# One core, four conditioned residual blocks: when ScalarE may read a bank of the first block, and how many units of the other work a step of the recurrence takes when that work is late

## The chip, the cores and the metric

The kernel runs on one core of a Trainium2 chip. The metric is the device time of one execution, in microseconds (us). Three runs of the kernel before the change took 1317.85 to 1319.22 us, with a median of 1318.93 us. One more execution was profiled; it took 1318.28 us, and its profile spans 1316.5 us from the first to the last instruction.

## The reference

The input is x of 8 sequences, 512 positions and 256 features, with one condition vector per sequence. Four residual blocks follow each other, x = x + block(x):

```
L0  s    = sigmoid(x @ router_w.T + cond @ router_t_w.T);  the two best of 8 experts, gates normalized
    out  = (silu(x @ sw1.T) * (x @ sw3.T)) @ sw2.T  +  sum_e gate_e * gelu(x @ rw1_e.T) @ rw2_e.T
    x    = x + out / 3
L1  a Haar transform scaled by gate(cond) and back: x * (a factor per sequence and feature)
L2  mid  = gelu(x @ base_down + (low rank, generated from cond));  x = x + mid @ base_up + (low rank)
L3  a GRU over the 512 positions, H of 8 x 256:
    Z = sigmoid(xz + H Whz), R = sigmoid(xr + H Whr), C = tanh(xh + (R*H) Whh), H = Z*H + (1-Z)*C
    x = x + H Whq + bhq
```

L0 to L2 treat every position by itself. L3 is a chain of 512 steps, each of which needs the one before.

## The kernel before

**Windows.** The 512 positions are cut into 16 windows of 32 (all 8 sequences together: 256 columns). `window_jobs` (line 497) writes down, for one window, everything of L0, L1 and L2 as a list of jobs; it runs nothing. Each job has an engine, the jobs that it depends on, the buffers that it uses and an assumed duration (`TAKES`). A product of 128 x 128 weights with 256 columns is one job of TensorE; `quads` (line 482) issues it as four matmuls of 32 output columns each. Such a job is called a unit (or a quad) here. In the profile every one of these matmuls has line 485, and a unit shows as x8 instructions, since a float32 matmul is recorded as two.

**Banks.** A hidden layer's tile in PSUM has 2 halves of 256 columns and fills one bank of 2 KB per partition (`r_h`, two of them; in window 0 every third one is `low`). `hidden` (line 557) makes the two units of one half. For the shared expert (lines 575 to 605) the first half holds x sw1 (units j0, j1) and the second x sw3 (j2, j3); ScalarE takes the sigmoid of the first half (line 583, tile `sig`) and VectorE makes two products (lines 591 and 599, tiles `lin` and `g`). For the routed experts (lines 607 to 642) the halves are two experts; ScalarE takes erf of each (line 617), VectorE makes `gl` (line 625), GpSimd multiplies by the gate that a DMA has spread over the partitions (line 634, tiles `bc` and `g`). `into_acc` adds two units per part to the window's sum `acc`. The framework orders accesses to PSUM by the bank, so a matmul into the second half that stands behind ScalarE's read of the first half in the program waits for that read.

**Two ways of ordering.** Ahead of the recurrence, `Jobs.run` (line 181) plays a clock in steps of 0.02 us and gives every engine the first job of its queue that is ready by the assumed durations; this carries windows 0 and a part of 1, the routing of the first four windows (`route`, line 903: logits on TensorE, some 25 small VectorE instructions, a transpose `cT` at line 939, a DMA to `comb_d` in DRAM at line 990, and from there by DMA into `bc` at line 517), the small products for the condition (line 1034) and the generation of the low-rank weights (`misc`, line 1104), which consumes eight loads of 1 MB. An engine's instructions are then issued in just this order, and each engine executes in order.

In the recurrence (lines 1362 to 1491) a step is written out by hand: the products of H for r and z on TensorE (line 1197, tiles `grh` and `gz`), ScalarE's gates (line 1379, `r`, `z`, `c`), VectorE's transposes (line 1393), the product R*H (line 1410), the products for the candidate (line 1197 with `s_rh`) and the scan that makes the new H (line 1469). Between them stand slots for the jobs of the windows. `first_slot` (line 1334) says how many units TensorE takes between the z products and the candidate's products, `second_slot` (line 1342) how many after those. `behind(s, by)` (line 1328) says whether more units are left than a straight line from the start to about step 462 allows, by more than `by`. In the first slot a late kernel takes a unit only if more than one is ready; in the second it takes two instead of one if the work is 8 units late (or late at all, in every second step) and more than two are ready. While window 1 isn't done (the first steps), both take what there is.

Of the kernel before, what the change touches and what calls it, by code (L numbers as in the profile page):

```python
# [18 lines left out]
KC = C // P  # L19
E = 8  # L20
# [40 lines left out]
PE_ALONE, PE_WOVEN = 0.43, 0.65  # L61
LEAD = 20
AHEAD = 1
RATE = 0.36
LAG = 3.5

# [137 lines left out]
def cond_resid_kernel(  # L204
# [173 lines left out]
    def load_sw13(k):  # L378
# [10 lines left out]
    rw1_sb = const.tile([P, KC, E, P], F32, name="rw1_sb")  # L389
    half = slice(0, E // 2), slice(E // 2, E)  # L390
    got_rw1 = [
        load(
            rw1_sb[:, :, e],
            rw1.rearrange("(k p) (e h) -> p k e h", p=P, h=P)[:, :, e],
            0.5,
        )
        for e in half
    ]
# [98 lines left out]
    def window_jobs(w, routed, xt, via_pool=False):  # L497

        add = jobs.add
        x = xw[w]  # L500

        def mm(lazy, n, lhs, rhs, start, deps, reads=(), tiles=NQ, takes=None):

            return add(
                "PE",
                lambda: quads(lazy.get()[: 32 * tiles, n], lhs(), rhs(), start, tiles),
                deps,
                [lazy, *reads],
                takes,
            )  # L510

        bcs = [Lazy(r) for r in r_bc]

        def fetch(i):
            (nc.gpsimd if via_pool else nc.sync).dma_start(
                out=bcs[i].get(),
                in_=comb_d[w : w + 1, 2 * i : 2 * i + 2].broadcast_to([P, 2, NT]),
            )  # L520

        fetched = [
            add(
                "POOL" if via_pool else "SP",
                lambda i=i: fetch(i),
                [routed[w % EARLY], got_w2 if w == 1 else None],
                [bcs[i]],
                1.0 if via_pool else None,
                lag=1.4 * LAG if via_pool else LAG,
            )  # L530
            for i in range(E // 2)
        ]

        acc = Lazy(r_acc)
        order = [None]

        def into_acc(part, lhs, deps, got):
            for m in range(KC):
                first = order[0] is None
                order[0] = mm(  # L540
                    acc,
                    m,
                    lambda m=m: lhs()[:, ts(m, P)],
                    lambda: part.get(),
                    first,
                    [*deps, got, order[0]],
                    [part],
                )

        turn = [0]  # L550

        def bank():

            turn[0] += 1
            return Lazy(r_low if w == 0 and turn[0] % 3 == 0 else r_h)

        def hidden(lazy, n, lhs, got, first=None):

            made = []
            for k in range(KC):  # L560
                made.append(
                    mm(
                        lazy,
                        n,
                        lambda k=k: lhs(k),
                        lambda k=k: x[:, k],
                        k == 0 and first is None,
                        [first, *made, got[k], got_x[w][k]],
                    )
                )  # L570
            return made

        later = []

        for m in range(HC):
            h, sig, lin, g = bank(), Lazy(r_sig), Lazy(r_lin), Lazy(r_g)
            j0, j1 = hidden(h, 0, lambda k, m=m: sw13_sb[:, k, 0, ts(m, P)], got_sw13)
            *_, j3 = hidden(
                h, 1, lambda k, m=m: sw13_sb[:, k, 1, ts(m, P)], got_sw13, j0
            )  # L580
            a = add(
                "ACT",
                lambda h=h, sig=sig: nc.scalar.activation(  # L583
                    sig.get(), h.get()[:, 0], AF.Sigmoid
                ),
                [j1],
                [h, sig],
            )
            d = add(
                "DVE",  # L590
                lambda h=h, sig=sig, lin=lin: tt(
                    lin.get(), h.get()[:, 0], sig.get(), ALU.mult
                ),
                [j1, a],
                [h, sig, lin],
            )
            d = add(
                "DVE",
                lambda h=h, lin=lin, g=g: tt(g.get(), h.get()[:, 1], lin.get(), ALU.mult),
                [j3, d],  # L600
                [h, lin, g],
            )
            later.append((g, lambda m=m: sw2_sb[:, m], [d], got_sw2))
            if len(later) > 2:
                into_acc(*later.pop(0))

        for e2 in range(0, E, 2):
            h, j0 = bank(), None
            for n in range(2):
                e = e2 + n  # L610
                got = [got_rw1[e // (E // 2)]] * KC
                j = hidden(h, n, lambda k, e=e: rw1_sb[:, k, e, :], got, j0)
                j0, j = j
                sig, gl, g = Lazy(r_sig), Lazy(r_gl), Lazy(r_g)
                a = add(
                    "ACT",
                    lambda h=h, sig=sig, n=n: nc.scalar.activation(  # L617
                        sig.get(), h.get()[:, n], AF.Erf, scale=RSQRT2
                    ),
                    [j],  # L620
                    [h, sig],
                )
                d = add(
                    "DVE",
                    lambda h=h, sig=sig, gl=gl, n=n: stt(
                        gl.get(), sig.get(), 1.0, h.get()[:, n], ALU.add, ALU.mult
                    ),
                    [j, a],
                    [h, sig, gl],
                    queue=None if w else jobs.small,  # L630
                )
                p = add(
                    "POOL",
                    lambda gl=gl, g=g, e=e: nc.gpsimd.tensor_tensor(  # L634
                        g.get(), gl.get(), bcs[e // 2].get()[:, e % 2], ALU.mult
                    ),
                    [d, fetched[e // 2]],
                    [gl, g, bcs[e // 2]],
                )
                later.append((g, lambda e=e: rw2_sb[:, e], [p], got_rw2))  # L640
                if len(later) > 3:
                    into_acc(*later.pop(0))
        for part in later:
            into_acc(*part)
        l0_ends.append(order[0])


        x1, x2, mid = Lazy(r_x1), Lazy(r_x2), Lazy(r_mid)
        turned = []
        halves = 2 if w < HALVED else 1  # L650
        for half in range(halves):
            at = slice(half * WS // halves, (half + 1) * WS // halves)
            turned.append(lower(w, at, acc, x1, x2, mid, xt, order[0]))
        return turned
# [184 lines left out]
    mu, j = mean_over_features(cond, got_cond)  # L839
    diff = set1.tile([P, KC, B], F32, name="diff")  # L840

    def center():
        for k in range(KC):
            tt(diff[:, k, :], cond[:, k, :], mu.get()[:, :B], ALU.subtract)

    j = dve(center, [j], [mu], 0.4)
    dsq = set1.tile([P, KC, B], F32, name="dsq")
    j = dve(lambda: tt(dsq, diff, diff, ALU.mult), [j])
    var_ps, j = mean_over_features(dsq, j)
    var = set1.tile([P, B], F32, name="var")  # L850
    j = dve(
        lambda: nc.vector.tensor_scalar(var, var_ps.get()[:, :B], EPS_LN, None, ALU.add),
        [j],
        [var_ps],
    )
# [5 lines left out]
    j = dve(  # L861
        lambda: tt(
            prod,
            rout[:, 1].rearrange("p k (o e) -> p k o e", o=1).broadcast_to([P, KC, B, E]),
            cond.rearrange("p k (b o) -> p k b o", o=1).broadcast_to([P, KC, B, E]),
            ALU.mult,
        ),
        [got_cond, got_rout],
    )
# [12 lines left out]
    j = pe(time_bias, [j], [tb_ps])  # L882
# [198 lines left out]
    for n, of in enumerate(LOW):  # L1081
# [15 lines left out]
        for k in range(KC):  # L1097
            got = [pieces[q, k] for q in of]
# [69 lines left out]
    with (  # L1168
# [159 lines left out]
        def behind(s, by=0):  # L1328
            return (
                any(j.done is None for j in ends[1][0])  # L1330
                or jobs.left("PE") > all_left * (LAST - s) / (LAST + LEAD) + by
            )

        def first_slot(s, at):

            if any(j.done is None for j in ends[1][0]) or jobs.ending() and jobs.left("PE"):
                return 1
            if jobs.left("PE"):
                return 1 if behind(s) and jobs.ready("PE", at + 1.0) > 1 else 0
            return 1 if len(jobs.last["PE"]) > T - s else 0  # L1340

        def second_slot(s, at):

            if not jobs.left("PE"):
                return 1
            two = behind(s, 8) or (s + 5) % 2 == 0 and behind(s)
            if two and (any(j.done is None for j in ends[1][0]) or jobs.ending()):
                return 2
            return 2 if two and jobs.ready("PE", at + 1.0) > 2 else 1
# [212 lines left out]
```

## Time and profile before

| what | us |
| --- | --- |
| median of three runs | 1318.93 |
| the profiled execution | 1318.28 |
| its span, first to last instruction | 1316.5 |
| before the first gate of step 0 (ScalarE's first `r`) | 67.77 |
| 511 steps from there to the first gate of the last step | 1241.18 |
| the rest: last step, last outputs | 7.55 |

The last three rows are read from the rows `ACT L1379 ACTIVATE r<-grh` of the trace, of which each step has two. The page gives per engine the busy time; TensorE is busy for 1178.3 us (89%), VectorE for 916.8 (70%), ScalarE for 505.7 (38%), GpSimd for 150.6 (11%). A row of the timeline gives start and duration in us, the engine (PE is TensorE's matmul, PEld its weight load, DVE VectorE, ACT ScalarE, POOL GpSimd, SPq the DMA queue that SyncE issues to), the line, the operation, output and input tiles, how many instructions are merged, and in brackets how long the engine was idle before and what released it. "issue" as a releaser means that the engine waited for nothing that the profile shows.

### The profile page before, as it was taken

Reading aid. Unit: us, or ns where it says so; the run is one execution under the profiler, and the core shown is the slowest. Engines: PE = TensorE matmul, PEld = TensorE weight load, DVE = VectorE, ACT = ScalarE, POOL = GpSimd, SP = SyncE. Lnnn points to the kernel's source line nnn. Section 1 sums busy time; section 2 is a strip of 40 time slices with the busy share of each in tenths; the row PEclk is TensorE's granted clock in tenths of the full one; section 3 lists DMA queues with packets and bytes.
Section 4 is the critical chain, followed back from the end, with each engine's and each line's share of the span. In section 5 each row is a group of like instructions: output and inputs, shape, how many; then the busy total and the mean of one; then the engine's idle time right before and its main releaser. Section 6 shows DMA issues by size and latency. Waiting matters only on the chain.

```text
span 1316.5 us, 88999 instructions
## 1 busy us (share of the span) xinstructions
PE 1178.3 (89%) x39240; PEld 688.4 (52%) x39240; DVE 916.8 (70%) x6271; ACT 505.7 (38%) x3407; POOL 150.6 (11%) x235
## 2 busy tenths in 40 slices
PE   8999999899999999998888988888888888878886
PEld 5666555555555555555554555545554545545443
DVE  5367777777776767676776767677676767667775
ACT  2134343444344444334343433443434344433332
POOL 3311110101011110101011010101101011110000
PEclk9999999999999999999999999999999999999999
DMA  9910001200010010100000010000001000000111
GB/s 318 352 53 16 5 4 38 52 5 29 13 36 20 12 29 5 52 4 28 12 15 26 4 36 4 22 19 12 28 4 29 12 4 4 4 4 4 36 30 26
DMA packets 41859, 46.46 MB, mean 35 GB/s; under 512 B 27488, under 2 KB 31104, under 8 KB 40320
## 3 DMA queue, kind: packets, MB, share of 16 engines
q1 hardware_dynamic: 38576, 38.31, 9.5%
q8 instruction: 306, 5.01, 1.6%
q0 software_dynamic: 1184, 2.31, 0.5%
q14 instruction: 81, 0.66, 0.2%
q10 hardware_dynamic: 1712, 0.16, 0.1%
HBM read 36.45 MB, written 4.33 MB: 31 GB/s over the span
## 4 chain that ended last, share of the span: by engine, by line
PE 66%; DVE 19%; ACT 9%; issue 4%; DMA 2%; SPq 0%; ACTq 0%
PE grh L1197 35%; PE hp L485 11%; DVE d L1393 7%; DVE rT L1393 6%; PE acc L485 6%; PE gz L1197 5%; ACT c L1379 5%; PE low L485 4%; ACT r L1379 4%; PE misc L485 3%; DVE s_h L1469 3%; DVE s_rh L1410 2%; DMA bc<-comb_d 1%; DMA sw_sb<-in_sw_dram 0%; PE misc L1104 0%
## 5 line engine op out<-in xcount | busy, mean ns | idle before, releaser
L1393 DVE STREAM_TRANSPOSE rT<-r 128x32 f32<-128x32 f32 x1024 | 156.1, 191 | 219.5 <-ACT r L1379 215.8
L1379 ACT ACTIVATE r<-grh 128x32 f32<-128x32 f32 x1024 | 146.3, 195 | 421.0 <-PE grh L1197 418.2
L1197 PE MATMUL grh<-wh,s_h 128*32 128x64 f32 x8192 | 221.8, 225 | 90.1 <-DVE s_h L1469 89.1
L1197 PEld LDWEIGHTS grh<-wh,s_h 128*32 128x32 f32 x8192 | 140.4, 109 | 309.6 <-DVE s_h L1469 308.4
L1379 ACT ACTIVATE c<-grh 128x32 f32<-128x32 f32 x1024 | 146.2, 195 | 313.6 <-PE grh L1197 313.1
L1197 PE MATMUL grh<-wh,s_rh 128*32 128x64 f32 x8192 | 221.6, 225 | 34.3 <-DVE s_rh L1410 10.0
L1197 PEld LDWEIGHTS grh<-wh,s_rh 128*32 128x32 f32 x8192 | 139.2, 108 | 191.8 <-DVE s_rh L1410 188.1
L1393 DVE STREAM_TRANSPOSE d<-c 128x32 f32<-128x32 f32 x1024 | 156.5, 192 | 115.2 <-ACT c L1379 108.9
L1197 PE MATMUL gz<-wh,s_h 128*32 128x64 f32 x8192 | 209.9, 219 | 0.4 <-issue 0.3
L1197 PEld LDWEIGHTS gz<-wh,s_h 128*32 128x32 f32 x8192 | 153.5, 110 | 0.9 <-issue 0.8
L485 PE MATMUL acc<-g,rw_sb 128*32 128x256 f32 x2048 | 153.5, 379 | 0.0
L485 PE MATMUL hp<-x,sw_sb 128*32 128x256 f32 x2016 | 150.8, 384 | 2.6 <-ACT sig L583 2.2
L634 POOL TENSOR_TENSOR g<-gl,bc 128x256 f32<-128x256 f32 x128 | 93.6, 733 | 511.9 <-DVE s_h L1469 358.8
L485 PE MATMUL hp<-x,rw_sb 128*32 128x256 f32 x2016 | 151.4, 380 | 0.7 <-ACT sig L617 0.6
L1469 DVE TENSOR_TENSOR_SCAN s_h<-d,d 128x16 f32<-128x16 f32 x1024 | 145.4, 184 | 0.0
L1410 DVE TENSOR_TENSOR s_rh<-rT,s_h 128x8 f32<-128x8 f32 x1024 | 133.5, 168 | 0.0
L1393 DVE STREAM_TRANSPOSE zT<-z 128x64 f32<-128x64 f32 x512 | 121.9, 238 | 0.4 <-ACT z L1379 0.3
L1379 ACT ACTIVATE z<-gz 128x64 f32<-128x64 f32 x512 | 121.4, 237 | 0.8 <-PE gz L1197 0.4
L1483 ACT COPY hist<-s_h 128x16 f32<-128x16 f32 x512 | 106.3, 208 | 0.5 <-DVE s_h L1469 0.5
L1197 PE MATMUL grh<-wx,xt 128*32 128x128 f32 x2048 | 104.8, 274 | 1.3 <-ACT r L1379 1.1
L1422 DVE TENSOR_TENSOR d<-zT,s_h 128x16 f32<-128x16 f32 x512 | 90.7, 177 | 17.5
L1423 DVE TENSOR_SCALAR d<-zT 128x16 f32<-128x16 f32 x512 | 86.8, 169 | 0.0
(154 smaller groups left out, 1208.7 us busy)
## 6 DMA issues: line engine op xcount, KB each, us to landing
bc<-comb_d SPq DMA_DIRECT2D x56, 256.0 KB, 3.2
w<-in_w_dram SPq DMA_DIRECT2D x5, 1024.0 KB, 13.5
out_dram<-x SPq DMA_DIRECT2D x14, 256.0 KB, 3.2
x<-in_w_dram SPq DMA_DIRECT2D x3, 1024.0 KB, 15.6
x<-in_xT_dram SPq DMA_DIRECT2D x2, 1536.0 KB
bc<-comb_d POOLq DMA_DIRECT2D x8, 256.0 KB, 9.0
sw_sb<-in_sw_dram SPq DMA_DIRECT2D x3, 512.0 KB, 8.0
wsq_a<-in_sq_a_dram SPq DMA_DIRECT2D x1, 1280.0 KB
```

Of the source, the lines that this page charges most:

```text
L485: nc.tensor.matmul(out[ts(j, 32)], lhs[:, ts(j, 32)], rhs, start=start, stop=False, skip_group_check=True,)
L634: lambda gl=gl, g=g, e=e: nc.gpsimd.tensor_tensor(g.get(), gl.get(), bcs[e // 2].get()[:, e % 2], ALU.mult),
L1197: nc.tensor.matmul(out[ts(j, 32)], lhs, rhs[:, ..., ts(j, FQ)], start=start, stop=False, skip_group_check=True,)
L1379: nc.scalar.activation(x, y, func)
L1393: ins = nc.vector.transpose(dst.rearrange("p i u b -> p i (u b)"), src.rearrange("p (i r) -> p i r", r=32),)
L1410: prod = tt(s_rh[u][:, k, u, :], rT[:, k, u, :], h[:, k], ALU.mult)
L1422: tt(d1[:, :, u, :, 1], zT[:, :, u, :], h, ALU.mult)
L1423: nc.vector.tensor_scalar(d0[:, :, :, 1], zT[:, :, u, :], -1.0, 1.0, ALU.mult, ALU.add)
L1469: new = nc.vector.tensor_tensor_scan(s_h[v][:, k, v].rearrange("p b w -> p (b w)"), d0[:, k].rearrange("p b w -> p (b w)"), d1[:, k, u].re ...
L1483: nc.scalar.copy(hist[:, :, t, :], s_h[v][:, :, v, :, 1])
```

## The change

Three edits. A constant `FAR = 16` is added, as line 64, so that all later lines move by one and more.

In window 0 (`w` is 0) ScalarE's read of a bank depends on the last unit of the bank's second half too, so that it is placed in the program behind both halves; in the other windows its dependencies are as they were.

For the routed experts the list of TensorE's jobs is written in another order, in all windows: the four units of a bank come first, and then what is added to `acc`; before, one part of `acc` stood between the two halves.

In the steps, when the work is more than 16 units late, the first slot takes one unit and the second two if so many are ready, without the conditions on how many are ready.

```diff
+FAR = 16
...
                 lambda h=h, sig=sig: nc.scalar.activation(
                     sig.get(), h.get()[:, 0], AF.Sigmoid
                 ),
-                [j1],
+                [j1, None if w else j3],
                 [h, sig],
...
         for e2 in range(0, E, 2):
-            h, j0 = bank(), None
-            for n in range(2):
+            h, j0, ends = bank(), None, []
+            for e in (e2, e2 + 1):
+                got = [got_rw1[e // (E // 2)]] * KC
+                j0, j = hidden(h, e % 2, lambda k, e=e: rw1_sb[:, k, e, :], got, j0)
+                ends.append(j)
+            for n, j in enumerate(ends):
                 e = e2 + n
-                got = [got_rw1[e // (E // 2)]] * KC
-                j = hidden(h, n, lambda k, e=e: rw1_sb[:, k, e, :], got, j0)
-                j0, j = j
                 sig, gl, g = Lazy(r_sig), Lazy(r_gl), Lazy(r_g)
                 a = add(
                     "ACT",
                     lambda h=h, sig=sig, n=n: nc.scalar.activation(
                         sig.get(), h.get()[:, n], AF.Erf, scale=RSQRT2
                     ),
-                    [j],
+                    [j, None if w else ends[1]],
                     [h, sig],
                 )
...
             if jobs.left("PE"):
+                if behind(s, FAR):
+                    return 1
                 return 1 if behind(s) and jobs.ready("PE", at + 1.0) > 1 else 0
...
             if not jobs.left("PE"):
                 return 1
+            if behind(s, FAR):
+                return 2
             two = behind(s, 8) or (s + 5) % 2 == 0 and behind(s)
```

## The prediction

> **What bounds the kernel now.** I read the chain of work that ended last first, then the timeline of the first 68 us, then the rows of the steps. The page's chain:
>
> ```profile
> PE 66%; DVE 19%; ACT 9%; issue 4%; DMA 2%; SPq 0%; ACTq 0%
> PE grh L1197 35%; PE hp L485 11%; DVE d L1393 7%; DVE rT L1393 6%; PE acc L485 6%; PE gz L1197 5%; ACT c L1379 5%; PE low L485 4%; ACT r L1379 4%; PE misc L485 3%; DVE s_h L1469 3%; DVE s_rh L1410 2%; DMA bc<-comb_d 1%; DMA sw_sb<-in_sw_dram 0%; PE misc L1104 0%
> ```
>
> The chain goes through the recurrence (`grh`, `rT`, `d`, `c`, `s_h`); the units of the windows (`hp`, `acc`, `low`) appear in it, so the question is whether they lengthen a step. I took the distance of the `r<-grh` rows for every step and set it beside the units that the program puts in it. It is 2.417 us for nearly all steps, with one unit in the second slot (median 2.417) as with two (2.419) or, in the early steps, three (2.418). So the span is 67.77 (first gate) + 511 x 2.417 = 1235.2 + 5.9 of extra time in single steps + 7.6 of end. A change of how many units a step takes moves nothing by itself; only the 67.8 us ahead and the 5.9 us of extras can move.
>
> Ahead of the recurrence TensorE works almost without pause, with these exceptions (timeline of the first 60 us; the engine's idle time stands in brackets):
>
> ```profile
> 16.68 0.64 PE L485 MATMUL low<-x,sw_sb 128*32 128x256 f32 x8 [0.51 <-ACT sig L583]
> ...
> 20.90 0.64 PE L485 MATMUL hp<-x,sw_sb 128*32 128x256 f32 x8 [0.57 <-ACT sig L583]
> ...
> 24.27 0.64 PE L485 MATMUL hp<-x,rw_sb 128*32 128x256 f32 x8 [0.56 <-ACT sig L617]
> ```
>
> Each is the last unit of a bank, which waits until ScalarE has read the first half. The extras have two kinds. One is TensorE without an instruction, here in step 59, which took 3.59 us:
>
> ```profile
> 216.47 0.35 PE L1197 MATMUL grh<-wh,s_h 128*32 128x64 f32 x9 [0.91 <-issue]
> ```
>
> The transfers of the instruction queue (16 KB each, usually 3.4 to 4.8 us apart) show one at 214.1, 6.2 us after the one before. The extras of steps 0 (1.33), 13 (0.46), 59 (1.17), 286 (0.34), 354 (0.12) and 232 (0.10) all lie at such a late transfer, 3.5 us together. The other kind is the wait inside a bank, as in step 163, of 2.60 us: the unit starts when VectorE's read ends.
>
> ```profile
> 466.12 0.42 DVE L625 SCALAR_TENSOR_TENSOR gl<-sig,hp 128x256 f32<-128x256 f32 x1 [0.21 <-PE hp L485]
> ...
> 466.60 0.64 PE L485 MATMUL hp<-x,rw_sb 128*32 128x256 f32 x8
> ```
>
> **First block.** The changed kernel's order on TensorE is the old one up to 26 us, except that the last unit of a bank no longer waits for ScalarE. Units follow each other every 0.43 us. The unit at 16.68 moves to 15.98 (two units after the start at 15.12: 0.70 earlier, more than the idle 0.51 because ends overlap), the one at 20.90 from 0.75 after its predecessor's place to directly behind it, likewise the one at 24.27 (0.76). Sum 2.2 us. The added wait costs ScalarE nothing: its sigmoid starts one unit (0.43) later relative to the bank, but before it already waited for the unit j2 (16.24, 0.08 after that ended), and TensorE arrives earlier; queued behind it on ScalarE are the routing's sigmoid and the next banks', with idle time of 1.2 to 3.0 us before each.
>
> What is late next? The loads: the DMA's ends in the trace are 17.2 for the first half of `rw1` (then used at 20.8), 22.4 for `wsq_a` (used at 23.9), 30.1 and 35.0 for the pieces of `w` (used at 32.9 and 38.8), so none comes into the way. VectorE's routing chain starts 0.7 earlier (its logits come after the first wait removed); two products of a bank now stand 3 instructions later in it, and it then waits, as before, for the product L1034, which comes at 23.9 instead of 26.13. So `cT` ends 2.2 earlier, and with it the gates' DMA (28.70) and the spreading one behind it on GpSimd:
>
> ```profile
> 34.24 2.21 POOL L517 DMA_DIRECT2D bc<-comb_d  x4 [4.75 <-DMA comb_d<-cT]
> ...
> 40.91 1.44 POOL L634 TENSOR_TENSOR g<-gl,bc 128x256 f32<-128x256 f32 x2 [4.46 <-DMA bc<-comb_d]
> ...
> 43.79 4.17 POOL L634 TENSOR_TENSOR g<-gl,bc 128x256 f32<-128x256 f32 x6 [1.44 <-DMA bc<-comb_d]
> ```
>
> If these land 2.2 earlier too, everything from there does, since TensorE ran without a wait from 39.3 to 54.5. The wait at 39.29 (0.56) belongs to window 1 and stays; so does the one of 1.11 at 57.59. Behind 55 us the changed order moves one unit of `acc` past the small products of window 1; I counted the units between two waits, 3 before and 3 after, so nothing is gained there, and the place where `acc` stood (58.05) becomes a wait for VectorE's `u`, which keeps its distance. The eighth piece of `w` is issued when the fourth is used (43.02) and lands at 47.9, used at 51.9; it moves along. First gate: 67.77 - 2.2 = 65.6.
>
> This price lies between 0 (another engine is late at once) and -2.8 (the wait at 39.29 goes as well). If the two transfers keep their landing (40.8 and 43.7), the third part of `acc` can't start before 44.6, one unit before the generation at 46.73 that then starts at 45.05 with the rest behind it: 1.3 instead of 2.2.
>
> **Order of the experts' units.** In the steps, the four units of a bank now stand together. Before, 70 units of the program waited for a read of the same bank by ScalarE or VectorE in the same step or the one or two before; in the changed order 27 do. Before, the steps with extras at such waits are 163 (0.18), 40 (0.10), 25 (0.06), 51 (0.03): 0.37. Taking away 43 of 70, those that cost most among them, I put down 0.3 (bounds 0 and 0.4). Of the units of `acc`, those that use a GpSimd product started only one step earlier fall from 12 to 4.
>
> **Slots of late steps.** By the order of the two programs, steps 0 to 27 take as many units as before; steps 28 to 47 take 57 instead of 48; the lead is 10 units at most, gone at step 160, and the windows' work ends at the same step, about 461. A third unit in a step costs 0 to 0.002 by the medians above, and fewer later units give nothing back, for those steps had 2.417 too: 0. If the units pulled ahead were not ready, TensorE would stand and the next `grh` behind it; the nearest row is again step 163, 0.18 each, so 0 to +1.6 for nine. SP's and GpSimd's queues keep one job per step.
>
> **Sum.** 1318.28 - 2.2 - 0.3 = 1315.8 for a profiled execution. That execution lay 0.65 under the median of the runs shown, so I give 1316.4 against 1318.93.
>
> **The Trainium skill.** "PSUM — Partial Sum Buffer", in the section on bank collisions, says that two engines must be kept apart by bank and 32-partition quadrant, whichever columns they touch; the wait of 0.57 between two halves of one bank agrees, so the change can't merely let both run, it has to pay for the order with a later read. "Runtime: NRT & Kernel Launch", section on instruction fetch, says that fetching is mostly hidden; by it the price of late instructions is 0 and the fourth case below falls away, but the 0.91 us above speaks against it.
>
> **Rivals.** First (forecast), 1316.4, chance 0.52, own range 1315.4 to 1317.4: the start moves by 2.2, the late instructions stay about as they were. Second, 0.18: the spreading transfers queue behind the loads of `w` and keep their landing; 1.3 + 0.3 gained, 1317.3. For it speaks that they took 6.5 and 9 us under that load; against it that the first packets came 3.7 us after the issue. Third, 0.15: the late instructions of step 0 (1.33) don't return, since the program lies otherwise against the 16 KB blocks: 1315.1. Fourth, 0.12, the other side: steps with three units issue more instructions in the same 2.417 us, so a late transfer empties TensorE more often. Place: steps 28 to 47. Price: about 1.2 each (steps 0 and 59). Two eat the gain, from the third on the kernel is slower: 1316.4 + 3.6 = 1320.0. In steps 0 to 27, which are as dense, two of 28 had one; that speaks for one event, not three. Fifth, 0.03: it doesn't do what it says, as other waits take the place of the removed ones at once: 1318.9.
>
> **Chances and range.** About 0.2% (2.64 us) is what a measurement of this kernel can tell from no change; that is 1316.3, just under the forecast. Faster by more: 0.25 of the first, 0.02 of the second, 0.15 of the third: 0.42. Slower by more: 0.04, of the fourth. Within: 0.54. The range for 8 in 10 takes in the first three and a part of the fourth: 1314.3 to 1319.0.
>
> **What would show it.** The three waits on `sig` at 16 to 25 us gone; the product L1034 near 23.9, first `bc` on GpSimd near 38.7 (40.9 would be the second case), first gate near 65.6; steps 28 to 47 at 2.42; waits of `hp` on ScalarE fewer; "issue" waits of TensorE of 3 to 4 us in the steps. A first gate later than 66.5, or extras in the steps over 7 us, would make the prediction wrong.

## The result, and the profile after

The changed kernel took **1320.28 us** (median of 22 runs, 1318.69 to 1322.41), the kernel before beside it 1318.35 us (22 runs). The ratio is 1.0014 (95% interval 1.0009 to 1.0020): slower by 0.14%, where 0.2% faster was forecast. The profiled execution took 1321.13 us. A second set of both kernels, told below, gave 0.9999; what both sets show alike is that the forecast gain isn't there.

| profiled execution | before | after |
| --- | --- | --- |
| first gate of step 0 | 67.77 | 67.70 |
| 511 steps to the last first gate | 1241.18 | 1243.57 |
| the rest | 7.55 | 8.06 |
| time over 2.417 us a step | 6.1 | 8.5 |

The chain of the page has the same links in the steps as before (loads of the start take a larger share of it), so the steps differ in waits and not in what bounds them:

```profile
PE 62%; DVE 19%; ACT 9%; DMA 4%; issue 4%; SPq 1%; POOL 0%; ACTq 0%; DVEq 0%; POOLq 0%
PE grh L1201 35%; PE hp L486 10%; DVE d L1401 7%; DVE rT L1401 6%; PE gz L1201 5%; ACT c L1387 5%; PE low L486 4%; ACT r L1387 4%; PE acc L486 4%; PE misc L486 3%; DVE s_h L1477 3%; DVE s_rh L1418 2%; DMA x<-in_w_dram 1%; DMA w<-in_w_dram 1%; DMA wh<-in_sq_b_dram 1%
```

**The start.** The three waits on `sig` between 16 and 25 us are gone; no row of TensorE has idle time on ScalarE there. The product L1038 comes at 23.71, as forecast (23.9), and GpSimd's row of the gates' DMA stands at 26.54, where it stood at 28.96 before. GpSimd's timeline shows what became of the 2.2 us:

```profile
26.54 0.53 POOL L994 DMA_DIRECT2D comb_d<-cT  x1 [12.78 <-DVE hid L1067]
33.56 2.21 POOL L518 DMA_DIRECT2D bc<-comb_d  x4 [6.50 <-DMA comb_d<-cT]
40.96 1.41 POOL L638 TENSOR_TENSOR g<-gl,bc 128x256 f32<-128x256 f32 x2 [5.18 <-DVE low_out L1124]
```

The gates' DMA was issued 2.4 us earlier than before, but GpSimd waits 6.50 us for it in the place of 4.75, and its first product starts at 40.96, where it started at 40.91 before. (The bracket names VectorE, but the first spreading transfer landed at 40.82, and in every profile this product starts 0.14 us behind that landing.) TensorE now has to wait for that product, and behind 62 us two more idle times stand in its timeline:

```profile
41.73 0.64 PE L486 MATMUL acc<-g,rw_sb 128*32 128x256 f32 x8 [0.92 <-POOL g L638]
...
63.60 0.64 PE L486 MATMUL hp<-x,sw_sb 128*32 128x256 f32 x8 [0.52 <-ACT sig L586]
...
64.49 0.40 PE L1201 MATMUL grh<-wx,xt 128*32 128x128 f32 x8
...
66.27 0.27 PE L1201 MATMUL grh<-wx,xt 128*32 128x128 f32 x1 [1.06 <-issue]
```

The products of x for step 0 start at 64.49, still 0.76 earlier than before. Then TensorE stands 1.06 us without an instruction, and the first gate is where it was. Before, the same place had 0.23:

```profile
66.17 0.42 PE L1197 MATMUL grh<-wx,xt 128*32 128x128 f32 x8 [0.23 <-issue]
```

The wait of 0.52 on `sig` is new too: all ten profiles with the first block's edit have it and none of the ten others. From the unit behind the wait of 1.11 (57.59 before, 56.15 now) to the products of x it is 7.66 us before and 8.34 now, so 0.68 of the gain is lost there.

**The steps.** Three kinds of extra time are new. First, VectorE's window work ahead of the gate's transpose, here in step 117 of 2.68 us:

```profile
355.30 0.41 DVE L602 TENSOR_TENSOR g<-hp,lin 128x256 f32<-128x256 f32 x1
355.63 0.29 DVE L1401 STREAM_TRANSPOSE rT<-r 128x32 f32<-128x32 f32 x2
...
358.04 0.30 DVE L1401 STREAM_TRANSPOSE rT<-r 128x32 f32<-128x32 f32 x2 [0.37 <-ACT r L1387]
```

The gate `r` began at 355.13 and 357.81; its transpose follows after 0.50 us in the first step and after 0.23 in the next, because `g` (355.30 to 355.71) stands ahead of it on VectorE. Second, a wait inside a bank in the second slot, in step 259 and then every 32 steps:

```profile
700.31 0.38 ACT L621 ACTIVATE sig<-hp 128x256 f32<-128x256 f32 x1 [0.21 <-PE hp L486]
...
700.75 0.16 PEld L486 LDWEIGHTS hp<-x,rw_sb 128*32 128x32 f32 x8 [0.18 <-ACT sig L621]
700.75 0.64 PE L486 MATMUL hp<-x,rw_sb 128*32 128x256 f32 x8
...
701.20 0.61 PE L486 MATMUL acc<-g,rw_sb 128*32 128x256 f32 x8
701.27 0.28 DVE L1477 TENSOR_TENSOR_SCAN s_h<-d,d 128x16 f32<-128x16 f32 x2
...
701.52 0.13 PEld L1201 LDWEIGHTS grh<-wh,s_h 128*32 128x32 f32 x4 [0.18 <-DVE s_h L1477]
```

The unit of `hp` waits 0.18 us until ScalarE has read the bank's other half; so the unit of `acc` behind it is still running (701.20 + 0.61) when the new H is ready and the next step's products want TensorE. It costs 0.095 us each time. In the steps of all seven profiles with the new order TensorE has 8 or 9 waits of over 0.15 us on `sig`; in the thirteen without it there is none. Third, the clock: in steps 474 and 475 the same product takes 0.65 us and then 0.43 us again,

```profile
1222.88 0.65 PE L1201 MATMUL grh<-wh,s_h 128*32 128x64 f32 x16 [0.22 <-DVE s_h L1477]
...
1226.04 0.43 PE L1201 MATMUL grh<-wh,s_h 128*32 128x64 f32 x16 [0.35 <-DVE s_h L1477]
```

for in this execution the granted clock was half of full speed for 3.41 us from 1222.05 on and again in the last step. That is 0.75 us in the two steps and some 0.6 at the end, half of what the two profiled executions differ by.

### The profile page after: what moved, and what is told of

Same layout as the page of the kernel before. It is cut to its first block, busy times and chain, and to the rows that moved or that the text cites. A ratio compares the mean times of both kernels' runs of the same rounds, so it can differ in the third digit from the quotient of the medians.

```text
span 1319.3 us, 89040 instructions
## 1 busy us (share of the span) xinstructions
PE 1180.6 (89%) x39240; PEld 689.5 (52%) x39240; DVE 915.0 (69%) x6271; ACT 507.2 (38%) x3407; POOL 150.6 (11%) x235
## 4 chain that ended last, share of the span: by engine, by line
PE 62%; DVE 19%; ACT 9%; DMA 4%; issue 4%; SPq 1%; POOL 0%; ACTq 0%; DVEq 0%; POOLq 0%
PE grh L1201 35%; PE hp L486 10%; DVE d L1401 7%; DVE rT L1401 6%; PE gz L1201 5%; ACT c L1387 5%; PE low L486 4%; ACT r L1387 4%; PE acc L486 4%; PE misc L486 3%; DVE s_h L1477 3%; DVE s_rh L1418 2%; DMA x<-in_w_dram 1%; DMA w<-in_w_dram 1%; DMA wh<-in_sq_b_dram 1%
## 5 line engine op out<-in xcount | busy, mean ns | idle before, releaser
L486 PE MATMUL hp<-x,rw_sb 128*32 128x256 f32 x2016 | 145.0, 380 | 0.2
```

Source lines behind the costliest of these rows:

```text
L486: nc.tensor.matmul(out[ts(j, 32)], lhs[:, ts(j, 32)], rhs, start=start, stop=False, skip_group_check=True,)
```

## The experiments

The time over 2.417 us a step was taken from the rows of `r`, as in the prediction. "Steps" below is the sum of the 511 steps of one profiled execution; medians and ratios are against the kernel before in the same set. Its own median lay between 1318.3 and 1319.9 us from set to set, so medians of different sets can't be compared to better than about 1.5 us.

**One part at a time.** The first block alone: ScalarE's dependence and the new order of units in window 0, in the other windows one half of a bank at a time as before, and no late slots (against the changed kernel).

```diff
-FAR = 16
+FAR = 10000
...
-            for e in (e2, e2 + 1):
...
+            for n in range(2):
...
+                while len(ends) < (2 if not w else n + 1):
+                    e1 = e2 + len(ends)
...
+                    ends.append(j)
```

> Only the first block is changed (ScalarE's reads behind both halves and the four units of a bank together, in window 0 alone). Theory A (what the start gains is eaten by late transfers of TensorE's instructions, and the units' order and the late slots bring the loss in the steps): the three waits on sig at 16 to 25 us are gone, the x products of step 0 start near 64.5 us, TensorE then stands about 1 us without an instruction near 66 us, first gate near 67.7; the steps' sum stays at 2 us of that of the kernel before, no clock of its own; ratio 0.999 to 1.001. Rival B (the first block itself brings the loss): first gate at 67.7 and the steps as long as in the changed kernel (1243.5), ratio 1.001 to 1.002.

1318.44 us (11 runs), ratio 0.9992 (0.9983 to 1.0001). First gate 66.47, products of x from 63.27 on, 1.06 us without an instruction at 65.05; steps 1242.49. The start is 1.3 us earlier than before and not at its old place as Theory A had it: in this execution GpSimd's first product began at 39.73, and TensorE waited only 0.18 us for it.

The order of units in windows 1 to 15 with the late slots, old first block. (The order without the late slots has no run; the late slots alone, below, tell the two apart.)

```diff
-                [j1, None if w else j3],
+                [j1],
...
-            for e in (e2, e2 + 1):
...
+                while len(ends) < (2 if w else n + 1):
...
-                    [j, None if w else ends[1]],
+                    [j],
```

> The order of the experts' units in windows 1 to 15 and the late slots, with the old first block. Theory A: first gate as before (67.8), the steps carry about 1.3 us of new waits of hp on ScalarE's sig, in steps that come every 32 (some 0.095 each), besides late instructions of 3 to 5 us; ratio 1.001 to 1.0025. Rival C (the loss in the steps is only chance in the instructions and the clock): no steps of 0.095 every 32, ratio 1.000.

1319.70 us (11 runs), ratio 1.0007 (0.9998 to 1.0016); first gate 66.91, steps 1243.21. Step 117 has its 0.261, steps 259, 291, 323, 355, 387 and 419 have 0.095 to 0.097, steps 459 to 461 have 0.344 (0.07 before). That is Theory A for the rows; the ratio alone, 0.9998 to 1.0016, would not exclude Rival C.

The late slots alone (the diff's last two hunks and nothing else):

> The late slots alone, in the old order of units and the old first block. Theory A: first gate 67.8, steps 28 to 47 at 2.42 as before, no row of 0.095 every 32 steps; ratio 0.9995 to 1.0005 up to the late instructions, which lie elsewhere. Rival D (the late slots bring the loss, by units that are not ready or by three units in a step): extras of 1 to 2 us more in steps 0 to 60, ratio 1.001.

1319.78 us (11 runs), ratio 0.9998 (0.9990 to 1.0007); steps 1242.71. None of the rows of the order; 5.7 us of late instructions, 1.88 of them in step 0, which the slots don't touch. The ratio says nothing at this noise.

**The same kernels once more,** unchanged:

> The kernel before, unchanged, profiled once more. Theory A: the instruction blocks end at the same instruction in each execution, so that TensorE stands at the same places of the program whenever the transfer is late; how late it is differs. The large ones (steps 0, 13, 59, 286) return where they depend on the loads that the program issues (0, 13), and those of 59 and 286 differ by up to 1 us. If all four return within 0.1 us, they are a property of the program. The granted clock halves for no more than 0 to 4 us ahead of the end.

1318.22 us; first gate 67.55, steps 1241.36. Steps 0 (1.61), 13 (0.34), 286 (0.46) and 354 (0.36, where it had 0.12) return, 59 does not; 68 (0.18), 73 (0.38), 132 (0.50) and 225 (0.59) are new. Late instructions have fixed places in the program, but which of them is late, and by how much, differs by execution.

> The changed kernel, unchanged, profiled and timed once more. Theory A: what comes from the order of the units returns to 0.01 us (step 117 with 0.26, steps 259 to 419 every 32 with 0.095, steps 460 and 461 with 0.14; 1.2 us in all more than the kernel before), the 1.06 us without an instruction ahead of the first gate returns too; the late instructions of the steps return in part, with other sizes; halves of the clock ahead of step 500 come or stay away by chance. First gate between 66.4 and 67.8, ratio 1.0005 to 1.002. Rival B (the loss is chance of one set of runs): ratio 0.999 to 1.000.

1320.00 us against 1319.73 (11 and 27 runs), ratio 0.9999 (0.9990 to 1.0008): in this set the change cost nothing that can be measured, so by the time Rival B holds. First gate 66.45, steps 1243.81. The rows are those of Theory A: those of the order return to 0.01 us, the 1.06 us ahead of the first gate too; the halves of the clock ahead of step 500 don't. GpSimd's rows of this execution against those of the first profile:

```profile
31.79 2.22 POOL L518 DMA_DIRECT2D bc<-comb_d  x4 [4.84 <-DMA comb_d<-cT]
38.15 1.43 POOL L638 TENSOR_TENSOR g<-gl,bc 128x256 f32<-128x256 f32 x2 [4.13 <-DMA bc<-comb_d]
```

The same DMA took 4.84 us here and 6.50 there, TensorE has no wait for GpSimd's product, and the start is 1.2 us earlier.

**Where the late instructions come from.** In the first pair GpSimd fills the gates' tile with 0.25 for windows 2 to 15 where SP issued a transfer of 256 KB:

```diff
         def fetch(i):
+            if w >= 2:
+                nc.gpsimd.memset(bcs[i].get(), 0.25)
+                return
```

> The changed kernel, in which the gates of windows 2 to 15 aren't spread by DMA: GpSimd fills the tile with the constant 0.25 in the place of each transfer, so the output is another. The 256 KB transfers of the steps (four per window) are gone. Theory A (late instructions come where these transfers stand ahead of an instruction transfer): from step 60 on no idle time of TensorE put down to issue is left, so the late instructions fall from some 3 us to the 1.5 us of steps 0 and 13; the waits of 0.095 and 0.26 stay; some 1.5 us less than the changed kernel, ratio 0.999 to 1.0005. Rival E (instructions are late of themselves, without other transfers): late instructions of 0.3 to 1 us in three to five steps from 60 on as before.

1317.79 us (11 runs), ratio 0.9989 (0.9981 to 0.9998); first gate 66.58, steps 1241.11. From step 30 on no idle time of TensorE on issue; 0.35 us of it in step 23. Step 64 took 0.71 us more, where four fills of GpSimd (1.93 us) stand beside VectorE instructions of up to 1.30 us; that is the experiment's own.

> The kernel before with the same constant in the place of the transfers of windows 2 to 15, so the output is another. Theory A: the late instructions from step 59 on (1.2 to 2 us) are gone, ratio 0.998 to 0.9995; the steps' sum near 1239. Rival E: sum 1240.5 to 1241.5 as before, late instructions in other steps.

1315.34 us (5 runs), ratio 0.9965 (0.9953 to 0.9978); steps 1238.10. No idle time on issue behind 70.3 us. So leaving these transfers out takes 4.4 us off the kernel before, more than the 3.5 us that the prediction had put down to late instructions in all, and Rival E falls.

In the next four nothing fills the tile (GpSimd reads one constant tile), so the parts can be seen without that lottery. All four ran in one set:

```diff
             if w >= 2:
-                nc.gpsimd.memset(bcs[i].get(), 0.25)
+                bcs[i].get()
                 return
...
-                        g.get(), gl.get(), bcs[e // 2].get()[:, e % 2], ALU.mult
+                        g.get(), gl.get(), (bcs[e // 2].get() if w < 2 else quarter)[:, e % 2], ALU.mult
```

> The kernel before without the gates of windows 2 to 15: their transfers are left out and GpSimd reads one tile filled once with 0.25, so the output is another; no engine has work in their place. This is the base for the three below. Theory A (from the earlier run with constants): about 4 us less than the kernel before, ratio 0.996 to 0.9975, no idle time put down to issue behind step 0.

> The same constants (so another output), with the edit of the first block alone. Without the transfers the late instructions of the steps are out of the way, so the edit's own price shows. Theory A: start 1.3 us earlier than in the base (the forecast 2.2 less 0.85 without an instruction near 65 us), nothing in the steps: 1.0 to 1.6 us below the base. Rival B (the edit brings loss to the steps): at or above the base.

> The same constants (so another output), with the order of the experts' units in windows 1 to 15 and the late slots, the old first block. Theory A: the new waits of hp on sig and of VectorE's order (step 117 0.26, 259 to 419 0.57, 460 and 461 0.28 and others) and late instructions in the dense steps 20 to 40 stay: 1.5 to 3 us above the base. Rival C (the loss in the steps is only chance in the late instructions behind the transfers): within 0.5 us of the base.

> The same constants (so another output), with all three edits. Theory A: the sum of the two above, 0.2 to 2 us above the base, since the gain of the first block and the loss of the order meet; the steps 0.7 us shorter than in the run in which GpSimd filled the tiles (step 64). Rival G (the edits disturb each other): more than 1 us off the sum of the two.

| with constant gates | median (runs) | ratio to before (95%) | first gate | steps |
| --- | --- | --- | --- | --- |
| kernel before | 1315.15 (5) | 0.9965 (0.9952 to 0.9977) | 66.38 | 1237.67 |
| first block | 1315.22 (5) | 0.9968 (0.9956 to 0.9981) | 66.57 | 1239.17 |
| order and late slots | 1316.90 (11) | 0.9979 (0.9970 to 0.9988) | 67.96 | 1239.78 |
| all three | 1316.91 (11) | 0.9982 (0.9973 to 0.9991) | 67.15 | 1240.64 |

The medians add up (0.07 + 1.75 against 1.76), which speaks against Rival G: order and late slots together cost 1.75 us, and the first block brings nothing. The intervals of the ratios overlap (each is 1.2 to 1.6 us wide to either side), so the medians alone don't prove it; the steps' sums, from one profile each, agree with them. What Theory A had not said is the second row: the first block's edit alone made the steps 1.5 us longer, by late instructions in steps 17 to 25 (0.17, 0.23, 0.52, 0.44). (The base's first gate is so early since its whole start ran 1.5 us earlier in that execution; from the first `low` unit, at 10.62, to the gate it takes 55.8 us, as the kernel before with 55.6; with the first block's edit it takes 54.5.)

**Why the first block makes instructions late.** The trace counts 2167 records of TensorE (weight loads and matmuls) ahead of the first gate in the kernel before and 2151 with the first block's edit: one unit, 16 records, slips behind the gate, and all that follows lies 16 records earlier against the transfers of instructions. Two kernels move it by 16 records alone. One clears half a bank twice at the start, in the first block's program with constant gates:

```diff
-    claim(gz.rearrange("p c n f -> p (c n f)"))
+    claim(gz.rearrange("p c n f -> p (c n f)"), (0, 0, 1))
```

> Constant gates for windows 2 to 15 (so another output) and the first block's edit, as in the run of that name, and four more matmuls on zeros at the very start (the first half of one bank is cleared twice), which puts every later instruction of TensorE 16 records further on, back to where the kernel before has them. Theory H (the position against the blocks of 256 instructions decides in which steps the instructions come late): the steps' sum falls from 1239.17 to within 0.4 of the base's 1237.67, the late ones of steps 9 to 25 are gone, 1 to 1.5 us less than the run without the shift. Rival I (the edit's other order of units in steps 5 to 29 does it): the sum stays at 1239.

1313.69 us (5 runs), ratio 0.9963 (0.9951 to 0.9975); first gate 66.65, steps 1237.91. The late instructions of steps 17 to 25 are gone (0.35 and 0.11 in 27 and 29 take their place), and TensorE doesn't stand ahead of the first gate. Step 23 in the first block's program and in the one moved by 16 records, in this order:

```profile
124.88 0.83 PE L488 MATMUL low<-x,wsq_a 128*32 128x128 f32 x21
125.98 0.52 PE L488 MATMUL low<-x,wsq_a 128*32 128x128 f32 x10 [0.28 <-issue]
126.23 0.29 PE L1210 MATMUL grh<-wh,s_h 128*32 128x64 f32 x5
```

```profile
124.34 1.08 PE L488 MATMUL low<-x,wsq_a 128*32 128x128 f32 x32
125.31 0.43 PE L1210 MATMUL grh<-wh,s_h 128*32 128x64 f32 x16
```

The same 32 matmuls run without a break, and the products of H start 0.97 us behind their start and not 1.35 us.

The other takes 16 records away from the base, by clearing a bank with four matmuls of 512 columns:

> The base with constant gates (so another output), in which one bank is cleared by four matmuls of 512 columns in the place of eight of 256, so every later instruction of TensorE lies 16 records earlier, where the first block's edit puts it. Theory H: late instructions of 0.15 to 0.5 us appear in steps 9 to 25, the steps' sum rises from 1237.67 to 1238.7 or more. Rival I: it stays at 1237.7.

1315.48 us (10 runs), ratio 0.9977 (0.9967 to 0.9986); steps 1240.01, of which 0.73 is a half clock (steps 473 and 510). Late instructions appear in steps 23 (0.48) and 25 (0.17), as with the first block's edit, and in 132 and 135. Theory H in both directions, by one profile each; the ratios (0.9963 against 0.9968, and 0.9977 against 0.9965) lie in each other's intervals. All profiles together say the same: step 25 has a late block, of 0.17 or 0.44 us, in all eight profiles of programs that lie 16 records earlier, and in none of the twelve others.

> Constant gates (so another output) with the late slots alone, the old order of units. Theory A (the order brings the waits, the slots do not): steps' sum 1237.7 to 1238.5, and the median within 0.7 us of the base. Rival D (the slots bring the 1.75 us of order and slots together): sum 1239 to 1240.

(The constants with the late slots alone.) 1315.12 us (8 runs), ratio 0.9974 (0.9964 to 0.9984); steps 1238.03, 0.36 more than the base and 1.75 less than with the order. So by the steps' sums the order brings the loss and the slots bring little; the ratios alone wouldn't settle it.

> The kernel before with the first block's edit alone and four more matmuls on zeros at the start, which put TensorE's instructions back by the 16 records that the edit had moved them; all transfers as before. Theory H: first gate 66.2 to 66.8, steps' sum as of the kernel before (1240.5 to 1242.5, with its scatter); 1 to 2 us less than the kernel before, ratio 0.9985 to 0.9993. Rival I: like the first block alone, 0.9992 or above.

(All transfers.) 1318.69 us (12 runs), ratio 1.0001 (0.9992 to 1.0010); first gate 66.50, steps 1242.68. A miss: the gate is as early as expected, and TensorE doesn't stand ahead of it, but steps 0 (1.99), 59 (1.29) and 131 (0.82) have late instructions. With the gates' transfers in the way, a shift moves the late ones and doesn't remove them.

**The transfers.** In the changed kernel, the last load of x (3 MB) is issued in six pieces in the first steps and not at 47.7 us; TensorE's program is the same:

```diff
-    load_x(NW - EARLY, 1.8)
+    load_x(NW - EARLY, 0.6, None, None, True)
...
+    for j in held_x:
+        j.deps.append(l0_ends[1])
```

> The changed kernel, in which the last load of x (3 MB for windows 4 to 15) isn't issued at 47.7 us but in six pieces in the first steps, once window 1 is done; TensorE's program is the same. Theory A (this load delays the instruction transfer that should have landed ahead of 64.8 us): the 1.06 us without an instruction near 66 us are gone, so is most of step 0's 1.06; first gate 0.8 to 1.1 earlier (66.6 if the spreading lands as in the profile of the changed kernel, 65.6 if as in the run with the first block alone), some of it lost again to late instructions in steps 4 to 15; ratio 0.9995 to 1.001. Rival F (the stand is due to the number of instructions alone): it stays at 1.06.

1320.78 us (11 runs), ratio 1.0009 (1.0000 to 1.0018); steps 1246.01. The 1.06 us ahead of the gate are gone: the products of x run from 64.20 without a break, and the gate comes 1.92 us after (3.21 in the changed kernel). Step 0's extra is gone as well. The load takes it back in steps 13 to 20, which have 5 us over 2.417 us each; in step 16 TensorE stands for 1.65 us:

```profile
109.17 0.24 PE L1216 MATMUL grh<-wh,s_rh 128*32 128x64 f32 x1 [1.65 <-issue]
```

Last, the transfers of the kernel before in smaller pieces: each gate transfer in two of 128 KB, a third of x at the old place and the rest in pieces of 256 KB behind windows 2 and 3:

```diff
-                out=bcs[i].get(),
+                out=bcs[i // cut].get()[:, i % cut * 2 // cut : (i % cut + 1) * 2 // cut],
...
+        if w in (2, 3):
+            for j in late_x[w - 1]:
+                j.deps.append(l0_ends[w])
```

> The kernel before, with the same instructions on TensorE, VectorE, ScalarE and GpSimd, and only SP's transfers in another form: each gate transfer of 256 KB in two of 128 KB, and of the last 3 MB of x only the third for windows 4 to 7 at the old place, the rest in pieces of 256 KB in the steps behind windows 2 and 3. Theory A (the length of a transfer decides how late the instructions come): step 0's 1.3 to 1.6 falls to 0.5 or less, the late instructions from step 59 on from 2 us to under 1; 1.5 to 3 us less than the kernel before, ratio 0.9978 to 0.999. Rival J (more transfers hit more instruction transfers): as many late instructions as before or more, ratio 1.000 or above.

1319.37 us (11 runs), ratio 1.0005 (0.9996 to 1.0014); steps 1243.09. A miss: step 0's extra is gone, but step 16 has 1.96 us, and the late instructions from 59 on sum to as much as before. Rival J's ratio holds. A likely reason, not tested, is that SP issues the two halves directly behind each other, so an instruction transfer meets the same 256 KB.

> The same transfers with the first block's edit and the four more matmuls at the start: no late slots, the old order of the experts' units. Theory A: first gate 65.7 to 66.6, steps' sum 1238.5 to 1240.5; 2 to 4 us less than the kernel before, ratio 0.997 to 0.9985. Rival J: 0.9995 or above.

(The same with the first block and the four more matmuls.) 1319.02 us (11 runs), ratio 0.9998 (0.9989 to 1.0006); steps 1242.50, with 1.43 in step 0 and 1.65 in step 16. A miss too. The gate came 53.4 us after the first `low` unit (10.86), the shortest of all; the kernel before needs 55.6. So ahead of the gate the forecast 2.2 us of the first block can be had, in this one profile with two thirds of the load of x moved, and they are lost again behind it.

No version with all transfers beat the kernel before beyond its interval; the first block alone (0.9992) came nearest.

## Why the prediction was wrong

**First block, −2.2: the waits went, and the gain was lost at three places that the sum put at nothing.** TensorE and the gates' DMA were on time up to 26.5 us. The step that failed is "If these land 2.2 earlier too, everything from there does". In its place the two profiles of the changed kernel have the gate 0.07 and 1.10 us earlier than the two of the kernel before.

First, two transfers scatter: the small one (4.84 and 6.50 us in the two executions of the changed kernel, 4.75 and 6.50 in those of the kernel before) and the first spreading one behind it (6.1 to 8.2 us from issue to landing over all profiles). When the first product of GpSimd is late by them, the second rival holds: `acc` waits 0.92 us in the first profile, 0.18 with the first block alone, and not at all in the second profile. (The prediction gives that rival 1.3 us; its own figures, 46.73 and 45.05, make 1.7.)

Second, where the prediction had "nothing is gained there" behind 55 us, the new wait on `sig` stands. In the second profile TensorE is 2.5 to 2.7 us ahead of the kernel before at the wait of 1.11, and only 1.8 to 2.0 at the products of x.

Third, the late instructions ahead of the gate take 0.83 more than before. I had let that idle time (0.23) move along with the rest. It doesn't: the transfer of that block starts 4.5 us after TensorE has passed the record that lies 268 ahead of the stop, where it was 2.9 to 3.1 before and is 1.6 with the load of x moved. So the load holds it up. But the shift by one unit is needed too: the two runs that put 16 records back, with the load at its old place, don't stand there. Why the two together make 4.5 us is not shown. What is left at the gate is 1.1 to 1.3 us.

**Order of units, −0.3: wrong in sign.** The step that failed is "Taking away 43 of 70, those that cost most among them, I put down 0.3": I counted how many units wait for a read of the same bank (70, then 27) and took the number for the price. All seven profiles with the new order have the same rows, to 0.01 us: step 117 with 0.26, six steps from 259 on with 0.095, steps 459 to 461 with 0.27 more than before; the thirteen without it have nothing there (but one 0.08 in step 355, a late block). That is 1.1 us. (The 0.28 that the late slots alone bring in step 469 is missing in them, so the last 0.27 may be the slots' as much as the order's.) In all five profiles with the three edits together six more steps (8, 38, 68, 100, 130, 194) have 0.09 to 0.10. Against that stand steps 163 and 40 (0.28), which the late slots alone remove as well. So in the changed kernel the term measured about +1.4 us in the place of −0.3. With constant gates the medians put order and slots together at 1.75 us. Few waits can cost more than many: what matters is whether TensorE or VectorE is late when the recurrence's next instruction is ready, as in the rows of step 259.

**Late slots, 0: about right.** 0.36 us by the steps' sums: steps 32 and 469 are longer (0.25 and 0.28, in both profiles of the slots alone), 40 and 163 shorter (0.28 together), and step 0 differs by 0.28. The fourth rival had a true mechanism at a wrong place and price: dense steps do get late instructions, but mostly in steps 17 to 29 (in 30 to 47 only 0.12 and 0.16 us, in steps 37 and 47 of one profile each), and 0.2 to 0.6 us each and not 1.2.

**"Issue" extras about as before: right in their sum, wrong in their cause.** In the steps they were 3.9 and 4.5 us in the two executions before, and 4.3 and 5.1 after (the extras over 0.08 us of steps in which a block of instructions landed less than 1.7 us ahead of its use, without step 4, which has 0.55 in every profile). But they belong to no step: they depend on 16 records of shift and on the gates' transfers. The third rival saw the shift as a gain; it may as well be a loss, and with constant gates it was one of 1.3 us by the steps' sums of one profile each, as much as the start gains.

**What no term had:** the half clock of the first profile (1.4 us of its 2.8). The part in steps 474 and 475 isn't a property of the change: the second profile doesn't have it, and the run that takes 16 records from the base has one in step 473. The time behind the last first gate is 8.1 us in both profiles of the changed kernel and 7.5 in those of the kernel before; the half clock at the end begins 0.2 to 0.5 us ahead of that gate there, and 1.8 us or more behind it here. That this makes the difference is likely and not shown.

**A sum.** 511 x 2.417 is 1235.1 and not 1235.2, so the extras before were 6.1 us and not 5.9; nothing hangs on it.

**What stays open.** The two sets of the unchanged pair gave 1.0014 (1.0009 to 1.0020) and 0.9999 (0.9990 to 1.0008), whose intervals just miss each other. With constant gates the loss is 0.13%; how late the instructions are with all transfers, set by set, I can't forecast. That the load of x holds the instruction transfer is shown by moving it; how the two share a queue was not tried.

## What to carry to other kernels

In a long unrolled program, TensorE's instructions are themselves a stream of transfers. An edit that moves the program by a few instructions, or a bulk load by a few microseconds, can change the time by as much as the edit is meant to gain; measure it with that traffic taken away before believing a gain of 0.1%. And weigh a wait by what the critical chain finds when it comes back, not by how often it occurs.

## What the runs showed of the hardware

**Instructions come in blocks of 256 records.** The 306 transfers of TensorE's instruction queue have 16 KB each, and there are 256.6 records of TensorE to one transfer. Where TensorE stands for a late block, it stops at record 449 + 256 i (the count of the kernel before; to the record where the stop is long), until block i has landed and some 1.4 us more: all 73 idle times of over 0.15 us put down to issue behind 60 us, in all profiles, end 1.19 to 1.65 us after such a landing. A transfer starts at the earliest when TensorE has passed record 181 + 256 i (181 to 188 over all profiles). Between the two lie 268 records, which is 4.0 us in the dense steps (160 records in 2.417 us); the transfer itself (1.0) and the 1.4 leave it 1.6 us to start. From that point the median to the transfer's start is 0.9 us. Behind step 20 the longest of a profile is 2.5 to 3.3 us with the gates' transfers, and 1.7 to 2.0 with constant gates (2.4 in one of those nine profiles). Beside the bulk loads of the start it is up to 4.8 us.

"Runtime: NRT & Kernel Launch", section "Instruction fetch mechanics", of the Trainium skill states blocks of 16 KiB, 256 instructions; the trace agrees (16 KB, 256.6 records). That the cost is mostly hidden holds for all but nine to thirteen of the 306 transfers in the steps of the four profiles of the two kernels; those cost 3.9 to 5.1 us.

**Half clocks come in pieces of 3.41 us.** In the profiles, stretches at half of full speed last 3.41 or 6.83 us at the start and 3.41 us late in the recurrence (steps 473 to 475 in two executions); each profile has another one from the last step or two on, which runs past the end. "TensorE: Matmul & The Clock Gate", section "What's actually happening", states a free-running window of 3413 ns; the trace agrees in the length.
